# Early statistics beside two stages, layer 1 and rows of the first sample placed closer, and the values' row of layer 3 added in the context

## The chip, the core and the metric

The kernel runs on one core of a Trainium2 chip. The core has a matrix engine (TensorE, PE in the profile; its weight loads are shown apart as PEld), a vector engine (VectorE, DVE), an activation engine (ScalarE, ACT), a general engine (GpSimd, POOL) and a synchronization engine (SyncE, SP), which here only issues DMA transfers. Each engine works through its own list of instructions in order and waits on semaphores for the others. The metric is device time in microseconds of one execution.

## The reference, cut to what matters

The input x is 16 samples of 4096 tokens (64 x 64) with 256 channels, in float32. Four layers follow one another, each of the form x = x + layer(group norm of x), with 32 groups over channels and all tokens of a sample. So every layer needs a whole sample's statistics before it can begin.

```
layer 0: indices = argmin(|xf|^2 + |E|^2 - 2 xf E)        # 1024 codes; the code's vector is added
layer 1: f, g, h = x Wf, x Wg, x Wh (with biases); out = sigmoid(f g^T) h   # over the 64 positions of a row
layer 2: sim = x0[:, None] * x1[None, :]; sm = softmax(sim, axis=1)         # 4096 x 4096 a sample
         gate = sigmoid(x2 sm); out = gate * x
layer 3: q, k, v = split(x w_qkv); q = softmax over a head's 32; k = softmax over tokens
         context = k v^T; out = layernorm((context q) w_out + b_out) * gamma + beta
```

## The kernel before, in words

A sample goes through stages, each a Python generator that yields after a piece of work:

- stats0 (lines 313 to 324): loads the sample's transposed input in 8 chunks of 512 KB (line 319, pool xb, 4 buffers), BN_STATS on DVE (line 266, two a chunk), and at the end gn_finish (lines 276 to 299), a short chain over PE, ACT and POOL that gives scale and bias.
- stage1, "search" (lines 329 to 436): 32 tiles of 128 tokens. Its loads are lines 338 (pool xa) and 342. A tile is the code distances on PE (line 403), the row term on ACT (line 398), maximum and index on DVE (lines 409 and 414), and a gather-and-add DMA issued by POOL (line 415). Per chunk of four tiles the result is transposed on PE (line 378), copied by ACT (line 381), given to BN_STATS and stored (line 384).
- layer1 (lines 441 to 562): 8 chunks. Loads at line 453 (pool xm), PE lines 482, 493, 498, 513 and 533, the add on DVE (line 538), BN_STATS, store at line 545.
- rows2 (lines 567 to 608) and spread_rows (610 to 618): the three rows x0, x1, x2 of layer 2 (line 590 loads through pool xb, line 593 multiplies, line 599 stores the rows, line 615 spreads them to all partitions).
- stage2, "exps" (lines 620 to 676): 64 times an exponential of 128 x 2048 on ACT (line 645) and a multiply-and-sum on DVE (line 648). Then gate2 (lines 681 to 714, line 695 reads the gate back, line 703 applies it).
- stage3, "layer 3" (lines 717 to 926). Its first half computes keys (line 765), queries and values together (line 782, two tiles to a PSUM bank, 128 columns of queries and 128 of values each), adds the row qv_row (the group norm's mean carried through the weights, in three bfloat16 parts) with a matmul of ones (line 786), and accumulates the context ctxa = exp(k) v over the chunks (lines 807, 809, 813). After the last chunk come ksum (line 827, the sum of exp(k) per key channel) and the small chain from the transposed context (line 832) to the output weights (lines 834 to 852).

The order of the work has two layers. A table of tasks with a start, a length and a number of pieces (lines 932 to 958) is run through a heap (lines 961 to 968): each task's next piece is traced when its virtual time comes; one unit is one sample's search. FILL (line 39) says in which stretches the statistics of samples 1 to 7 are traced: two passes in 0.05 to 0.95, three in 1.0 to 1.27, two in 1.4 to 1.58. The constants LAG1, LEN1, LAGR, LAG2 place layer 1, rows and exps behind one another; for sample 0 layer 1 begins at 1.06 and has length 0.2, the rows have 0.1, the exps follow 0.17 later. The framework then schedules the traced instructions onto the engines' lists, with what stands under tc.high_priority (gn_finish and the small chains) drawn forward. What results is a fixed list for each engine, SP's list of DMA issues among them: a load that has to wait for its buffer holds up all loads behind it.

Of the kernel before, what the change touches and what calls it, by code (L numbers as in the profile page):

```python
# [2 lines left out]

# [32 lines left out]
LAG3, LENG = 0.06, 0.8  # L36
LAG4 = 0.04
LEN3 = {0: 0.4, 1: 0.33, 2: 0.37}
FILL = ((0.05, 0.95, 2), (1.0, 1.27, 3), (1.4, 1.58, 2))
EARLY = sum(n for _, _, n in FILL)  # L40


@with_exitstack
def kernel(
# [263 lines left out]
                engine.tensor_scalar(v, v, scale[:, k : k + 1], None, ALU.mult)  # L308


    norm0 = {}

    def stats0(b):
        tag = f"s0_{b}"
        st = stats_tile(0, f"st_{tag}")
        src = xT[b].rearrange("(k p) n -> p k n", p=P)
        for ch in range(NCHUNK):
            xt = xb.tile([P, NK, CW], F32, tag="xb", name=f"xs_{tag}_{ch}")
            nc.sync.dma_start(out=xt, in_=src[:, :, ch * CW : (ch + 1) * CW])
            chunk_stats(st, xt, ch)  # L320
            yield 1.5
        with tc.high_priority(offset=URGENT):
            norm0[b] = gn_finish(st, "n0", b)
        yield 2


    x1_d, norm1 = {}, {}

    def stage1(b):
# [5 lines left out]

        def load(ch):
            xt[ch] = xa.tile([P, NK, CW], F32, tag="xa", name=f"xt_{tag}_{ch}")
            nc.sync.dma_start(out=xt[ch], in_=src[:, :, ch * CW : (ch + 1) * CW])

        def tokens(ch):  # L340
            xc[ch] = s1p.tile([P, CH, C], F32, tag="xc", name=f"xc_{tag}_{ch}")
# [51 lines left out]
        for ch in range(NCHUNK):  # L393
            for t in range(CH):
                T = ch * CH + t

                nn = s1p.tile([P, CODES], F32, tag="t4", name=f"nn_{tag}_{T}", bufs=3)
                nc.scalar.activation(nn, ne2, AF.Identity, bias=nx2[ch][:, t : t + 1])  # L398
                pd = wide(f"pd_{tag}_{T}")
                for hf in range(2):  # L400
                    cols = slice(hf * 512, (hf + 1) * 512)
                    for k in range(NK):
                        nc.tensor.matmul(  # L403
                            pd[:, cols], lhsT=xn[ch][:, k, t * P : (t + 1) * P], rhs=e2[:, k, cols],
                            start=(k == 0), stop=(k == NK - 1),
                        )

                m8 = m8s[T % 4]
                nc.vector.tensor_tensor_reduce(  # L409
                    out=nn, in0=pd, in1=nn, scale=1.0, scalar=-3.0e38, op0=ALU.add, op1=ALU.max,  # L410
                    accum_out=m8[:, 0:1],
                )
                i8 = small.tile([P, 8], U32, tag="i8", name=f"i8_{tag}_{T}", bufs=4)
                nc.vector.max_index(i8, m8, nn)  # L414
                nc.gpsimd.indirect_dma_start(  # L415
                    out=xc[ch][:, t, :], out_offset=None,
                    in_=emb_rows, in_offset=bass.IndirectOffsetOnAxis(ap=i8[:, 0:1], axis=0),
                    compute_op=ALU.add,
                )
                yield 4  # L420
                if t == 1 and ch > 0:
                    back(ch - 1)
                    yield 2
                if t == 2 and ch + 1 < NCHUNK:
                    norm(ch + 1)
                    yield 2
                if t == 3:
                    if ch + 1 < NCHUNK:
                        norm_rows(ch + 1)
                        tokens(ch + 1)  # L430
                    if ch + 2 < NCHUNK:
                        load(ch + 2)
# [8 lines left out]
    def layer1(b):  # L441
# [8 lines left out]

        def load(ch):
            xt[ch] = xm.tile([P, NK, CW], F32, tag="xm", name=f"xt_{tag}_{ch}")
            nc.sync.dma_start(out=xt[ch], in_=x1[ch])

        load(0)
        load(1)
# [93 lines left out]
        for ch in range(NCHUNK):  # L550
            if ch > 0:
                store(ch - 1)
            if ch + 1 < NCHUNK:
                yield from attend(ch + 1)
                yield 2
            mix(ch)
            yield 3
        store(NCHUNK - 1)

# [157 lines left out]
    def stage3(b):  # L717
# [40 lines left out]
        for ch in range(NCHUNK):  # L758
# [18 lines left out]
            for pr in range(CH // 2):  # L777
                pqv = bank(f"pqv_{tag}_{ch}_{pr}").rearrange("p (j n) -> p j n", j=2)
                for j in range(2):
                    t = 2 * pr + j  # L780
                    for k in range(NK):
# [1 line left out]
                            pqv[:, j, :], lhsT=xt[:, k, t * P : (t + 1) * P], rhs=wqv_n[:, k, :],  # L783
                            start=(j == 0 and k == 0), stop=False, skip_group_check=True,
                        )
                nc.tensor.matmul(pqv, lhsT=ones3, rhs=twice(qv_row), start=False, stop=True, skip_group_check=True)
                nc.scalar.copy(qv[:, 2 * pr : 2 * pr + 2, :, :].rearrange("p j s n -> p j (s n)"), pqv)
            if ch == 0:
                put_row(x_row, xm_, by_identity, f"x_{tag}", idle=8)
# [39 lines left out]
        nc.vector.reciprocal(rk, ksum)  # L829
        with tc.high_priority(offset=URGENT):  # L830
            pt = bank(f"pct_{tag}")
            nc.tensor.transpose(pt[:, :P], ctxa, ident)
            ctx_bd = wts.tile([P, P], F32, tag="ctx_bd", name=f"ctxbd_{tag}")
            nc.vector.tensor_tensor(ctx_bd, pt[:, :P], hmask, ALU.mult)
# [95 lines left out]


    tasks, free = [], {}
    b = 0
    for begin, end, n in FILL:
        for k in range(n):
            b += 1
# [9 lines left out]
    for b in range(nb):  # L946
# [1 line left out]
        if b > EARLY:  # L948
            tasks.append((b - 0.7, 0.5, stats0(b), 14))
        task("search", b, 1.0, stage1(b), 160)  # L950
        end = task("layer1", b + 1 + LAG1, (LEN1 if b else 0.2) if left else 0.35, layer1(b), 88)
        task("rows", end + LAGR, 0.1, rows2(b), 8)
        if left:
            end = task("exps", end + LAG2, 1.0, stage2(b), 160)
            end = task("gate", end + LAG3, 0.15 if left == 1 else LENG, gate2(b), 36)
        else:
            end = task("exps", end + LAG2, 0.65, stage2(b, NCHUNK), 200)
# [47 lines left out]
```

## Time and profile before

| | |
|---|---|
| median of 3 runs | 5679.94 us (5666.18 to 5681.68) |
| profiled execution | 5674.06 us |
| its span, first to last instruction | 5672.1 us |
| mean granted TensorE clock | 0.962 |
| instructions | 76096 |
| DMA | 1059.26 MB, 187 GB/s over the span |

The page gives, for each engine, busy time, share of the span and number of instructions. Matmuls are pipelined, and their recorded ends are modelled, so a PE that is shown busy is not PE at its peak. Two more views are used. One cuts the span into stretches and gives each engine's busy time in them, with the granted clock, the mean busy share of the 16 DMA engines and what they moved. The other lists who waited for whom: engine, line, what released it, total us, times, longest us. An f32 matmul of the code stands in the trace as two records.

Where the stages of the first two samples stand in the profiled execution (first and last start of their main instructions, us):

| stage | sample 0 | sample 1 |
|---|---|---|
| search (DVE line 409) | 39 to 177 | 184 to 480 |
| layer 1 (DVE line 538) | 216 to 289 | 540 to 673 |
| rows (PE line 593) | 298 to 313 | 685 to 702 |
| exps (DVE line 648) | 333 to 590 | 718 to 1000 |
| layer 3, first half (PE line 765) | 831 to 987 | 1296 to 1436 |

### The profile page before, as it was taken

What the parts mean: (1) busy time and instruction counts of PE and PEld (TensorE: products, weight loads), DVE (VectorE), ACT (ScalarE), POOL (GpSimd) and SP (SyncE); (2) the same over time, 40 slices, a digit from 0 to 9 for tenths busy, and PEclk for the clock granted to TensorE, in tenths of its full rate; (3) what the DMA queues carried; (4) which work ended last, traced back from release to release, by engine and by line L of the source; (5) the groups of instructions that cost most, each with busy time, mean ns of one, the idle gap of its engine ahead of it and who ended that gap; (6) DMA issues with size and microseconds to landing.
All of it is one profiled execution on the core that took longest, in us unless ns stands there. A gap on an engine that the chain in (4) does not pass through costs nothing.

```text
span 5672.1 us, 76096 instructions
## 1 busy us (share of the span) xinstructions
PE 5162.0 (91%) x26927; PEld 3189.6 (56%) x26927; DVE 5049.3 (89%) x7186; ACT 4571.1 (81%) x6642; POOL 1801.5 (32%) x1076
## 2 busy tenths in 40 slices
PE   7977889989999999999999999999999999987788
PEld 3534446545656566565655656565565656564556
DVE  7589799899999999999999999999999999988882
ACT  4468589888989898888978888898888879887873
POOL 2223234323333333334333333333333333321221
PEclk9988999999999999999999999999999999998889
DMA  8553744655665757566575656657575675745543
GB/s 254 174 178 84 232 115 144 214 163 185 196 198 175 224 159 236 171 211 198 185 234 155 216 185 200 210 173 236 160 224 183 201 219 156 222 149 176 200 157 119
DMA packets 521365, 1059.26 MB, mean 187 GB/s; under 512 B 52504, under 2 KB 266392, under 8 KB 512792
## 3 DMA queue, kind: packets, MB, share of 16 engines
q1 hardware_dynamic: 406288, 885.11, 46.5%
q0 software_dynamic: 73728, 67.14, 8.3%
q10 hardware_dynamic: 40968, 102.13, 4.6%
q8 instruction: 214, 3.51, 0.3%
q14 instruction: 167, 1.37, 0.1%
HBM read 751.18 MB, written 303.04 MB: 186 GB/s over the span
## 4 chain that ended last, share of the span: by engine, by line
PE 46%; DVE 17%; ACT 16%; issue 6%; DMA 5%; POOL 4%; SPq 0%; ACTq 0%; DVEq 0%; POOLq 0%
PE pd_s L403 14%; ACT ex_s L645 7%; DVE ex_s L648 7%; PE ph_l L493 4%; PE pxo_s L908 3%; PE pqv_s L782 3%; PE po_l L533 2%; PE pk_s L765 2%; ACT nn_s L398 2%; POOL qv_s L802 2%; PE pz_s L857 2%; DVE i_s L414 2%; DVE nn_s L409 2%; PE pxo_s L902 2%; PE pvr_s L865 2%
## 5 line engine op out<-in xcount | busy, mean ns | idle before, releaser
L648 DVE CUSTOM_DVE_ANT_0 ex_s<-ex_s,x2b 128x2048 f32<-128x2048 f32 x1024 | 2360.4, 2312 | 77.6 <-ACT ex_s L645 74.6
L645 ACT ACTIVATE ex_s<-x0b,nmax_s,x_r 128x2048 f32<-128x2048 f32 x1024 | 2138.6, 2089 | 40.7 <-DVE num_s L648 30.5
L403 PE MATMUL pd_s<-e,xn_s 128*128 128x512 f32 x4096 | 1971.1, 614 | 43.9 <-DVE m L409 27.9
L415 POOL DMA_INDIRECT xc_s<-in_emb_rows,i_s x512 | 1113.7, 2175 | 1852.7 <-DVE i_s L414 1337.5
L403 PEld LDWEIGHTS pd_s<-e,xn_s 128*128 128x128 f32 x4096 | 745.8, 195 | 778.8 <-issue 669.1
L409 DVE CUSTOM_DVE_ANT_0 nn_s<-pd_s,nn_s 128x1024 f32<-128x1024 f32 x512 | 619.9, 1212 | 113.5 <-PE pd_s L403 63.0
L414 DVE FIND_INDEX8 i_s<-m,nn_s 128x8 uint32<-128x1024 f32 x512 | 622.9, 1217 | 0.0
L398 ACT ACTIVATE nn_s<-ne,nx_s 128x1024 f32<-128x1024 f32 x512 | 582.5, 1143 | 33.1 <-DVE nx_s L369 18.7
L493 PE MATMUL ph_l<-wh_l,xt_l 128*128 128x256 f32 x2048 | 519.6, 390 | 28.7 <-DVE m L409 16.9
L782 PE MATMUL pqv_s<-wqv_s,xk_s 128*128 128x256 f32 x2048 | 489.3, 381 | 0.0
L493 PEld LDWEIGHTS ph_l<-wh_l,xt_l 128*128 128x128 f32 x2048 | 379.7, 192 | 138.9 <-issue 69.0
L782 PEld LDWEIGHTS pqv_s<-wqv_s,xk_s 128*128 128x128 f32 x2048 | 389.1, 191 | 120.6 <-issue 59.7
L802 POOL TENSOR_TENSOR qv_s<-qv_s,qm_s 128x512 f32<-128x512 f32 x128 | 221.6, 1731 | 662.6 <-DVE qm_s L801 363.2
L868 POOL TENSOR_TENSOR lrs_s<-lrs_s,mhalf 128x4 f32<-128x4 f32 x128 | 178.0, 1391 | 677.2 <-ACT lrs_s L867 663.3
L756 POOL TENSOR_TENSOR qv_s<-qv_s,qd_s 128x512 f32<-128x512 f32 x128 | 214.4, 1675 | 249.0 <-DVE qd_s L755 132.0
L533 PE MATMUL po_l<-blk,h_l 128*128 128x128 f32 x2048 | 282.1, 288 | 3.0 <-DVE m L409 1.5
L533 PEld LDWEIGHTS po_l<-blk,h_l 128*128 128x128 f32 x2048 | 260.6, 200 | 41.1 <-issue 24.5
L908 PE MATMUL pxo_s<-wctx_s,qo_s 128*128 128x256 f32 x1024 | 269.2, 386 | 2.2 <-DVE qo_s L876 2.2
L765 PE MATMUL pk_s<-xk_s,wk_s 128*128 128x512 f32 x512 | 256.0, 620 | 1.0 <-DMA xk_s<-x_g 0.9
L913 ACT COPY y_s<-pxo_s 128x512 f32<-128x512 f32 x256 | 147.5, 580 | 132.4 <-PE pxo_s L912 116.0
L378 PE MATMUL pt_s<-ident,xc_s 128*128 128x128 f32 x1024 | 156.7, 282 | 105.2 <-DMA xc_s<-in_emb_rows,i_s 79.0
L351 ACT ACTIVATE sq_s<-xt_s,first 128x512 f32<-128x512 f32 x256 | 200.2, 806 | 37.2 <-DMA x0b<-rows_r 21.0
(206 smaller groups left out, 7322.0 us busy)
## 6 DMA issues: line engine op xcount, KB each, us to landing
xs_s<-in_xT SPq DMA_DIRECT2D x128, 512.0 KB
xt_s<-in_xT SPq DMA_DIRECT2D x128, 512.0 KB
xc_s<-in_x SPq DMA_DIRECT2D x128, 512.0 KB
x_s<-xt_s ACTq DMA_DIRECT2D x128, 512.0 KB
xt_l<-x_s SPq DMA_DIRECT2D x128, 512.0 KB
x_l<-xt_l SPq DMA_DIRECT2D x128, 512.0 KB
xr_r<-x_l SPq DMA_DIRECT2D x128, 512.0 KB
xg_g<-x_l SPq DMA_DIRECT2D x128, 512.0 KB
```

The source lines that it names most:

```text
L398: nc.scalar.activation(nn, ne2, AF.Identity, bias=nx2[ch][:, t : t + 1])
L403: nc.tensor.matmul(pd[:, cols], lhsT=xn[ch][:, k, t * P : (t + 1) * P], rhs=e2[:, k, cols], start=(k == 0), stop=(k == NK - 1),)
L409: nc.vector.tensor_tensor_reduce(out=nn, in0=pd, in1=nn, scale=1.0, scalar=-3.0e38, op0=ALU.add, op1=ALU.max, accum_out=m8[:, 0:1],)
L414: nc.vector.max_index(i8, m8, nn)
L415: nc.gpsimd.indirect_dma_start(out=xc[ch][:, t, :], out_offset=None, in_=emb_rows, in_offset=bass.IndirectOffsetOnAxis(ap=i8[:, 0:1], axis=0),
L493: nc.tensor.matmul(ph[:, t, :], lhsT=X[:, k, t * P : (t + 1) * P], rhs=wh_n[:, k, :], start=(t % 2 == 0 and k == 0), stop=False, skip_grou ...
L533: nc.tensor.matmul(po[:, m : m + P], lhsT=h[:, t, k * P : (k + 1) * P], rhs=at[:, t, :, :].rearrange("p r i -> p (r i)"), start=True, stop ...
L645: nc.scalar.activation(ex, x0b, AF.Exp, bias=nmax[:, T : T + 1], scale=x01[:, T, 1:2], accum_out=den[:, h, T : T + 1])
L648: nc.vector.tensor_tensor_reduce(out=ex, in0=ex, in1=x2b, scale=1.0, scalar=0.0, op0=ALU.mult, op1=ALU.add, accum_out=num[:, h, T : T + 1],)
L765: nc.tensor.matmul(pk, lhsT=wk_n[:, k, :], rhs=xt[:, k, :], start=(k == 0), stop=(k == NK - 1))
L782: nc.tensor.matmul(pqv[:, j, :], lhsT=xt[:, k, t * P : (t + 1) * P], rhs=wqv_n[:, k, :], start=(j == 0 and k == 0), stop=False, skip_group ...
L908: nc.tensor.matmul(px[:, j, :], lhsT=qT[:, t * P : (t + 1) * P], rhs=wctx[:, 1, :], start=False, stop=False, skip_group_check=True,)
```

## The change

It has three parts. First, the statistics of samples 1 and 2 are no longer traced by virtual time but piece by piece beside the search of sample 0, from within its loop over tiles, and those of samples 3, 4 and 5 beside layer 1 of sample 0, from within its loop over chunks. Their loads are traced under `issue_after(marks[...])`, where the mark is the last load that the search or layer 1 has issued: on SP they stand behind it. The statistics of samples 6 and 7 move from 1.4 to 1.58 to 2.62 to 3.04. Second, for sample 0 alone, layer 1 is placed at 1.02 with length 0.12, its rows get length 0.04, and the exps follow 0.08 behind them. Third, the matmul of ones that adds qv_row covers only the queries' 128 columns of each tile. The values' part of the row is added once, to the context: every value had the same row added, so the context gains ksum times that row. A matmul of ones spreads the row into the PSUM bank of the transposed context, and one DVE operation adds ksum times it to ctxa before the transposition.

```
-FILL = ((0.05, 0.95, 2), (1.0, 1.27, 3), (1.4, 1.58, 2))
-EARLY = sum(n for _, _, n in FILL)
+FILL = ((2.62, 3.04, 2),)
+BESIDE = (2, 3)
+EARLY = sum(BESIDE) + sum(n for _, _, n in FILL)
...
-    norm0 = {}
-
-    def stats0(b):
+    norm0, marks = {}, {}
+
+    def behind(name):
+
+        return tc.issue_after(marks[name]) if name in marks else nullcontext()
+
+    def stats0(b, after=None):
...
-            nc.sync.dma_start(out=xt, in_=src[:, :, ch * CW : (ch + 1) * CW])
+            with behind(after):
+                nc.sync.dma_start(out=xt, in_=src[:, :, ch * CW : (ch + 1) * CW])
...
+    beside = {
+        "search": chain.from_iterable(stats0(b, "search") for b in range(1, 1 + BESIDE[0]) if b < nb),
+        "layer1": chain.from_iterable(stats0(b, "layer1") for b in range(1 + BESIDE[0], 1 + sum(BESIDE)) if b < nb),
+    }
+
+    def advance(name, b, n):
+
+        for _ in range(n if b == 0 else 0):
+            next(beside[name], None)
...
-            nc.sync.dma_start(out=xt[ch], in_=src[:, :, ch * CW : (ch + 1) * CW])
+            marks["search"] = nc.sync.dma_start(out=xt[ch], in_=src[:, :, ch * CW : (ch + 1) * CW]).ins
...
                 yield 4
+                advance("search", b, ((T + 1) * 9 * BESIDE[0]) // NT - (T * 9 * BESIDE[0]) // NT)
...
-            nc.sync.dma_start(out=xt[ch], in_=x1[ch])
+            marks["layer1"] = nc.sync.dma_start(out=xt[ch], in_=x1[ch]).ins
...
             mix(ch)
+            advance("layer1", b, ((ch + 1) * 9 * BESIDE[1]) // NCHUNK - (ch * 9 * BESIDE[1]) // NCHUNK)
...
-                nc.tensor.matmul(pqv, lhsT=ones3, rhs=twice(qv_row), start=False, stop=True, skip_group_check=True)
+                nc.tensor.matmul(
+                    pqv[:, :, 0:P], lhsT=ones3, rhs=twice(qv_row)[:, :, 0:P], start=False, stop=True, skip_group_check=True
+                )
...
             pt = bank(f"pct_{tag}")
+            nc.tensor.matmul(pt[:, P : 2 * P], lhsT=ones3, rhs=qv_row[:, P:], start=True, stop=True)
+            nc.vector.scalar_tensor_tensor(ctxa, pt[:, P : 2 * P], ksum, ctxa, op0=ALU.mult, op1=ALU.add)
             nc.tensor.transpose(pt[:, :P], ctxa, ident)
...
-    b = 0
+    b = sum(BESIDE)
...
-        end = task("layer1", b + 1 + LAG1, (LEN1 if b else 0.2) if left else 0.35, layer1(b), 88)
-        task("rows", end + LAGR, 0.1, rows2(b), 8)
+        end = task("layer1", b + 1 + (LAG1 if b else 0.02), (LEN1 if b else 0.12) if left else 0.35, layer1(b), 88)
+        task("rows", end + LAGR, 0.1 if b else 0.04, rows2(b), 8)
...
-            end = task("exps", end + LAG2, 1.0, stage2(b), 160)
+            end = task("exps", end + (LAG2 if b else 0.08), 1.0, stage2(b), 160)
```

## The prediction

> **What bounds the kernel now.** I read the page's engine totals first, then the busy time by stretch, cut where a stage of an early sample begins or ends; the cuts are first and last starts of the stage's lines. Columns: stretch, its length, then busy us and (instructions) of PE, weight loads, DVE, ACT and POOL, then the granted clock, the DMA share and GB/s.
>
> ```profile
> PE 5162.0 (91%) x26927; PEld 3189.6 (56%) x26927; DVE 5049.3 (89%) x7186; ACT 4571.1 (81%) x6642; POOL 1801.5 (32%) x1076
> ```
>
> ```profile
> 39.00:177.00 138.00, 126.45 (x463) 58.89 (x462) 121.67 (x211) 67.24 (x89) 50.50 (x35) 0.99 0.84 243
> 177.00:290.00 113.00, 104.66 (x705) 68.19 (x704) 54.45 (x90) 51.27 (x99) 16.86 (x15) 0.95 0.49 153
> 290.00:333.00 43.00, 36.47 (x146) 16.15 (x145) 25.55 (x50) 15.59 (x28) 12.00 (x12) 0.93 0.84 290
> 333.00:590.00 257.00, 189.77 (x773) 95.91 (x772) 244.68 (x314) 210.98 (x254) 78.32 (x36) 0.87 0.37 105
> 590.00:718.00 128.00, 113.93 (x554) 59.09 (x553) 85.61 (x146) 67.64 (x104) 30.34 (x22) 0.97 0.80 253
> 718.00:1016.00 298.00, 278.16 (x1416) 162.97 (x1414) 272.30 (x378) 262.42 (x371) 103.63 (x55) 0.96 0.47 143
> ```
>
> The rows are: search of sample 0; its layer 1; its rows; its 64 exponentials; the gap to the second sample's exponentials; those. No one engine sets the pace. Search 0 is PE (92%) with DVE behind it (88%) and much DMA; layer 1 is PE (93%) while DVE is half idle; the exponentials of sample 0 are DVE (95%) while PE is starved; the gap is PE and DMA. From 718 on PE and DVE are both over 90% and a sample takes some 330 us. The start is where engines take turns in waiting; the steady part has little slack anywhere.
>
> How the order moves I read from the built programs' instruction orders. Tile (s,t) is the t-th of the 32 search tiles of sample s on DVE. Layer 1 of sample 0 (its eight chunk adds) stands behind tiles (1,2) to (1,7) before, behind (1,0) to (1,3) after. The first exponential product of sample 0 stands behind (1,13) before, behind (1,6) after; its last behind (2,11) before, (2,4) after. The first product of sample 1 stands behind (2,29) in both. From the second sample's layer 3 on both orders are the same but for part three. So the start is decided by when (2,29) is reached, 718 now.
>
> **Part 1, the early statistics.** Within search 0 DVE runs 60 of their BN_STATS before, 34 after (676 ns each by its rows): 26 x 0.68 = 17.6 us less of DVE's 121.7. This does not set the end there; PE does, and it can win only its idle 138 - 126.5 = 11.5 us. Two waits tell how much of that the statistics cause (window 40 to 177; who waited for what, total us, times, longest), and one of SP's own (0 to 700):
>
> ```profile
> ACT xn_s L348 <- DMA xt_s<-in_xT: 12.9, 5, 3.0
> PE pt_s L378 <- DMA xc_s<-in_emb_rows,i_s: 11.5, 7, 2.9
> ```
>
> ```profile
> SPq L319 <- DVE st_s L266: 97.7, 39, 7.6
> ```
>
> SP issues in order. A statistics load (L319) that waits for a buffer which DVE has to free holds up the search's own load (L338) behind it, and ACT then waits for that. After, each statistics load stands behind the search load just issued. The gathers (L415), for which PE waits, share the 84% DMA with 13 fewer statistics loads. I take half of the 11.5: **-6**; bounds 0 and -11.5.
>
> The passes of samples 3 to 5 move into layer 1: 42 BN_STATS there instead of 16, 26 x 0.68 = 17.6 us more, on a DVE busy 54 of 113 us, where PE hides them. Their loads are 13 x 0.52 MB = 6.8 MB more on 153 GB/s x 113 us = 17.3 MB. The passes of samples 6 and 7 leave the rows and exponentials of sample 0 (8 in front of the first product, 24 behind it, 32 x 0.68 = 21.7 us of a saturated DVE) and go to tiles (2,4) to (2,31), where DVE is busy 86 of 128 us.
>
> **Part 2, layer 1 and rows closer.** Layer 1 loses four tiles of filler. A tile costs PE 8 records 0.43 us apart and some 0.4 us of transposes and row sums (L378: 156.7 us for 512 tiles), 3.8 us: 113 - 15 = 98. Its 24.1 MB less 2 MB of tiles in 98 us are 225 GB/s; the highest of the rows above is 290, so it fits, but SP's loads and stores of a chunk (L453, L545) now have statistics loads ahead of them that wait for buffers. I put 6 us on that (bounds 0 and 24, a 3 us landing wait per chunk as the longest 3.0 above): 104, **-9**. The rows' stretch is a chain of round trips: last BN_STATS 288.7, row matmuls 298 to 313, spread rows, first exponential on ACT at 322.3. Fewer search tiles inside it do not shorten it. Only the 10 us between 322.3 and DVE's first product at 332.7, spent on BN_STATS of sample 6 and search tiles, goes: **-10**. Exponentials begin at 333 - 6 - 9 - 10 = 308.
>
> The exponentials' stretch holds 30 tiles in both orders. DVE's 244.7 loses 24 BN_STATS (16.2) and three chunk adds of sample 1's layer 1 with their statistics (1.21 + 2 x 0.68 each, 7.7): 221, at 95% 232 us. End at 540, where it was 590.
>
> What is late next is PE. The gap to (2,29) now holds 25 tiles where it had 18, and eight chunks of layer 1 where it had five. A chunk costs PE 16 x 0.216 + 2 x 0.216 + 16 x 0.112 and about 1.7 for the small matmuls, 7.3 us. That is 7 x 3.8 + 3 x 7.3 = 48 us more: 176 us at the old 89% busy, and the 50 us are given back (540 + 176 = 716). With no exponentials beside layer 1, the nearest row is 177 to 290, PE 93% busy: 169 us, second exponentials at 709, **-9** on 718. Bounds: 716, and 690 if PE also loses the gate's round trip that the chain of waits shows at 598 to 618. DMA leaves little more: 253 x 128 us = 32.4 MB, plus 3.7 for tiles, 3.1 for chunks, 6.8 for 13 statistics loads is 46 MB, 159 us at the 290 GB/s of the row above.
>
> The Trainium skill, "DMA: Bandwidth & Descriptors", section Bandwidth, measures 425 GB/s for a core alone with large transfers; by that estimate the 46 MB take 108 us, DMA bounds nothing there, and the sum would be up to 19 us lower. No stretch of this trace reaches that rate.
>
> Behind 718, layer 3 of sample 0 starts eight tiles or so earlier; the work moves from a stretch where DVE bounds (1016 to 1312: DVE 281, PE 266 of 296) into one where PE is 93% busy. I cost it at 0, bounds +10 and -8.
>
> **Part 3, the values' row.** 256 matmuls of 512 columns become 256 columns. In the order of time (start, us, engine, line) the next matmul starts 0.21 us behind one:
>
> ```profile
> 836.89 0.38 PE L786 MATMUL pqv_s<-qv_row,ones 128*128 128x512 bf16 x1
> 837.10 0.81 PE L782 MATMUL pqv_s<-wqv_s,xk_s 128*128 128x256 f32 x3
> ```
>
> The 0.38 is its latency, the 0.21 what it costs in a stream; half of 0.215 (the other rows' spacing) is 0.108 saved, 27.5 us in all. How much of that shows depends on what else is full. Busy time in the nine stretches from the first to the last start of L765, layer 3's first half, samples 0 to 8:
>
> ```profile
> sum 1300.00, PE 1237.77 PEld 762.88 DVE 1193.06 ACT 1143.03 POOL 474.54; mean PE 137.53 PEld 84.76 DVE 132.56 ACT 127.00 POOL 52.73
> ```
>
> PE 95%, DVE 92%, ACT 88%: PE is the fullest, not the only one. I count three quarters: -21. Added per sample: a 128-column matmul (0.05 us, a quarter of 0.215, to 0.33, the latency of L832) and one DVE operation:
>
> ```profile
> L809 DVE SCALAR_TENSOR_TENSOR ctx_s<-ctx_s,al_s,pc_s x112: 325/342/350, 871.4 to 5614.9; 128x128 f32<-128x128 f32 x112
> ```
>
> It has the same form as the new one: 16 x 0.34 = 5.5 us of DVE, and the transposition of the context (L832) now waits for it with search matmuls queued behind it on PE, and DVE's L409 behind those. It waits for ksum, which is ready. I put +3 on it, bounds 0 and +12 (16 x (0.34 + 0.38)). **Sum -18**, bounds -27 and +12 if PE's saving is hidden.
>
> The Trainium skill ("Trainium Kernel Development and Optimization", Best Practices) judges PE by the share of weight loads, not of matmuls; in those nine stretches that is 762.9 of 1300, 59%. By that rule PE has room, the saving is hidden, and the part is worth about +3.
>
> **Sum.** -9 - 18 = -27 on the profiled execution's 5674.1 (span 5672.1 and 2 around it): 5647. The median of the three runs shown, 5679.9, lies 6 above it; I set the forecast midway between the two footings, **5650**.
>
> **Rivals.** (a) The gap keeps PE's waiting down: second exponentials at 690, -28, and part three whole, -27 + 3: 5674 - 52, about 5622. For: DVE is freed of 24 us in its saturated stretch. Against: DMA at 80% already. (b) The start gives all back (716 or later) and part three is half hidden or wholly: 5663 to 5680. For: PE's work to (2,29) is the same in both orders, only idle time can be won. (c) Slower: layer 1 of sample 0 is set by its transfers. If its 22.1 MB run at 175 GB/s it takes 126 us; the exponentials begin at 333 - 6 + 13 - 10 = 330, the gap ends at 330 + 232 + 176 = 738, +20, the earlier layer 3 adds its +10 and part three is hidden, +3: about 5707. It decides from 196 GB/s downward (22.1 MB in more than 113 us). For: the stage runs at 153 now, and SP waits for buffers. Against: 243 GB/s in search 0. That the change does not do what it says is excluded: the built order shows every statistics load behind its search load.
>
> **Numbers.** Forecast case 0.48, (a) 0.14, (b) 0.23, (c) 0.15. The 8-in-10 range is 5615 to 5690. What a measurement tells from no change here is 0.3%, 17 us: faster means under 5663. The forecast case lies under it mostly (0.44 of 0.48), (a) wholly, (b) hardly (0.01): faster 0.59. Slower, over 5697, is most of (c): 0.13. The rest is 0.28.
>
> **What would show it.** Search 0 ends near 171 and ACT's waits for L338's loads shrink; the first exponential product at about 308, the last at 540, DVE 95% between; sample 1's first product at 709 (690: rival a; 716 or more: b or c); DMA in the gap at 250 to 290 GB/s; the values' row 0.108 us apart and PE's busy share in layer 3's first half one point lower with the stretch 1 to 2 us shorter. Wrong if layer 1 of sample 0 takes over 113 us, or if steady samples keep their present distance.

## The result, and the profile after

The changed kernel is slower. Its median is 5719.6 us (six runs, 5713.4 to 5733.4) beside 5681.1 us for the kernel before (six runs); the ratio is 1.0071, 95% interval 1.0057 to 1.0085. The forecast was 5650 us with a range of 5615 to 5690: the change went the other way, and the time lies above the range. The profiled execution of the changed kernel has a span of 5715.3 us, 43 more than before.

The engine totals of the changed kernel, in the same form as before:

```profile
PE 5160.3 (90%) x26943; PEld 3178.4 (56%) x26943; DVE 5065.6 (89%) x7202; ACT 4560.5 (80%) x6642; POOL 1822.4 (32%) x1076
```

PE, DVE and ACT are the old ones within 0.4%, POOL has 1.2% more. The 27.5 us that the halved matmul of ones was to save do not show in PE's total. PE stands idle 555 us where it was 510: the 43 us are waiting. Where it sits is told by the busy time by stretch, cut at the same events as before: search, layer 1, rows and exponentials of sample 0, the gap, and then from the first exponential product of sample 1 to that of sample 2, and on to that of sample 3. Columns: stretch, length, PE, weight loads, DVE, ACT, POOL with instructions, granted clock, DMA share, GB/s.

```profile
41.00:175.00 134.00, 124.44 (x452) 58.06 (x451) 107.65 (x187) 66.63 (x87) 49.29 (x33) 0.99 0.67 185
175.00:279.00 104.00, 94.01 (x660) 63.34 (x659) 55.83 (x91) 43.10 (x90) 11.63 (x14) 0.93 0.62 207
279.00:316.00 37.00, 34.62 (x118) 12.98 (x119) 13.52 (x30) 8.85 (x18) 7.27 (x9) 0.91 0.66 216
316.00:540.00 224.00, 158.88 (x538) 73.16 (x530) 221.76 (x273) 201.81 (x230) 80.43 (x32) 0.87 0.35 95
540.00:720.00 180.00, 170.05 (x882) 92.37 (x880) 128.48 (x222) 94.23 (x151) 42.95 (x34) 0.98 0.80 254
720.00:1035.00 315.00, 289.79 (x1535) 177.34 (x1536) 283.99 (x389) 261.68 (x376) 113.86 (x59) 0.96 0.49 151
1035.00:1338.00 303.00, 257.75 (x1265) 145.58 (x1263) 277.86 (x371) 256.46 (x343) 80.42 (x44) 0.91 0.55 173
```

The first five rows add up to what they were (720 against 718): the exponentials of sample 0 end 50 us earlier, and the gap takes the 50 us back, with PE busy 94% of it. The last two rows are new losses, 315 where it was 298 and 303 where it was 296. The row before that answers to the last one is

```profile
1016.00:1312.00 296.00, 266.43 (x1388) 156.76 (x1388) 280.69 (x376) 257.94 (x350) 88.01 (x47) 0.95 0.60 189
```

Some 120 PE records (a part of layer 3 of sample 0) have gone from this stretch into the one ahead of it. The one ahead grew by 17 us, and this one, relieved, did not shrink.

First exponential product of a sample, from the profiled executions (us; search 0 and the exponentials of sample 0 by their first start and last end, here and in the table of before, where the last start lies 1 to 2 us earlier; the second row is the kernel before profiled once more, run e12, to show how far two executions differ):

| kernel | search 0 | sample 0 | sample 1 | 2 | 3 | 5 | 7 | 13 |
|---|---|---|---|---|---|---|---|---|
| before | 39 to 177 | 333 to 590 | 718 | 1016 | 1312 | 1955 | 2623 | 4633 |
| before again | 42 to 181 | 338 to 597 | 726 | 1028 | 1324 | 1971 | 2642 | 4655 |
| after | 41 to 175 | 316 to 540 | 720 | 1035 | 1338 | 2007 | 2685 | 4685 |
| part one alone (e3) | 39 to 171 | 335 to 572 | 706 | 1012 | 1307 | 1958 | 2632 | 4640 |
| part two alone (e4) | 39 to 177 | 316 to 558 | 732 | 1045 | 1345 | 1992 | 2660 | 4672 |
| e7 | 38 to 174 | 321 to 563 | 736 | 1039 | 1337 | 1985 | 2654 | 4661 |
| e8 | 41 to 179 | 357 to 600 | 713 | 1010 | 1311 | 1958 | 2630 | 4643 |

Two executions of one kernel differ by up to 22 us at a late stage, so single stage times are read only where they differ by more, or agree over several kernels.

### The profile page after: what moved, and what is told of

It reads as the page before. It is cut to its first block, busy times and chain, and to the rows that moved or that the text cites. A ratio compares the mean times of both kernels' runs of the same rounds, so it can differ in the third digit from the quotient of the medians.

```text
span 5715.3 us, 76199 instructions
## 1 busy us (share of the span) xinstructions
PE 5160.3 (90%) x26943; PEld 3178.4 (56%) x26943; DVE 5065.6 (89%) x7202; ACT 4560.5 (80%) x6642; POOL 1822.4 (32%) x1076
## 4 chain that ended last, share of the span: by engine, by line
PE 49%; DVE 18%; ACT 14%; DMA 7%; issue 6%; POOL 5%; ACTq 0%; SPq 0%; DVEq 0%; POOLq 0%
PE pd_s L420 16%; DVE ex_s L667 7%; ACT ex_s L664 6%; PE ph_l L511 5%; PE pxo_s L931 3%; PE pqv_s L801 3%; DVE i_s L431 3%; PE po_l L551 2%; PE pk_s L784 2%; POOL qv_s L823 2%; DVE nn_s L426 2%; PE pxo_s L925 2%; PE pz_s L880 2%; ACT nn_s L415 2%; DMA qo_s<-qd_s 2%
## 5 line engine op out<-in xcount | busy, mean ns | idle before, releaser
L432 POOL DMA_INDIRECT xc_s<-in_emb_rows,i_s x512 | 1158.3, 2262 | 1886.8 <-DVE i_s L431 1288.1
L823 POOL TENSOR_TENSOR qv_s<-qv_s,qm_s 128x512 f32<-128x512 f32 x128 | 208.5, 1629 | 655.1 <-DVE qm_s L822 465.1
L395 PEld LDWEIGHTS pt_s<-ident,xc_s 128*128 128x128 f32 x1024 | 120.8, 145 | 193.6 <-DMA xc_s<-in_emb_rows,i_s 115.5
```

Source lines behind the costliest of these rows:

```text
L432: nc.gpsimd.indirect_dma_start(out=xc[ch][:, t, :], out_offset=None, in_=emb_rows, in_offset=bass.IndirectOffsetOnAxis(ap=i8[:, 0:1], axis=0),
```

## The experiments

Each ratio is to the kernel before, run beside it on the same chip, with its 95% interval.

### The parts alone

**e1, part three alone:** the kernel before with the two edits of layer 3.

```
-                nc.tensor.matmul(pqv, lhsT=ones3, rhs=twice(qv_row), ...)
+                nc.tensor.matmul(pqv[:, :, 0:P], lhsT=ones3, rhs=twice(qv_row)[:, :, 0:P], ...)
...
+            nc.tensor.matmul(pt[:, P : 2 * P], lhsT=ones3, rhs=qv_row[:, P:], start=True, stop=True)
+            nc.vector.scalar_tensor_tensor(ctxa, pt[:, P : 2 * P], ksum, ctxa, op0=ALU.mult, op1=ALU.add)
             nc.tensor.transpose(pt[:, :P], ctxa, ident)
```

> The kernel before with the third part alone (the values' row added in the context). Theory A (the loss of 39 us is the start's order, above all that sample 0's layer 3 and exponentials stand earlier): the third part is worth what the steady samples of the changed kernel show, 0 to -18 us on 5681, so 5663 to 5681. Theory B (the third part itself costs, by the wait of the context's transposition and of the row chains behind it): 5695 or more, with the distance from the exponentials of sample 3 to those of sample 5 grown from 643 us to over 660.

Measured: 5695.5, 1.0040 (1.0024 to 1.0057); from sample 3's exponentials to sample 5's 671 us. This is what theory B said.

**e2, the changed kernel without part three** (the same edit undone).

> The changed kernel without the third part: the statistics and the sample 0 placement stay. Theory A: as slow as the changed kernel or slower, 5715 to 5740; the exponentials of sample 2 start near 1035, those of sample 5 near 2005. Theory B: 5680 to 5700.

Measured: 5709.9, 1.0067 (1.0045 to 1.0089), between the two theories. Sample 2 begins at 1037 as theory A had it, sample 5 at 1991 and not near 2005.

**e3, part one alone:** the statistics beside search 0 and layer 1, the lags as before. **e4, part two alone:** the lags.

```
-        end = task("layer1", b + 1 + LAG1, (LEN1 if b else 0.2) if left else 0.35, layer1(b), 88)
-        task("rows", end + LAGR, 0.1, rows2(b), 8)
+        end = task("layer1", b + 1 + (LAG1 if b else 0.02), (LEN1 if b else 0.12) if left else 0.35, layer1(b), 88)
+        task("rows", end + LAGR, 0.1 if b else 0.04, rows2(b), 8)
...
-            end = task("exps", end + LAG2, 1.0, stage2(b), 160)
+            end = task("exps", end + (LAG2 if b else 0.08), 1.0, stage2(b), 160)
```

> The kernel before with the first part alone (statistics of samples 1 to 5 beside search and layer 1, 6 and 7 at 2.62). Theory A, if the exponentials' earlier place is the cause: 5670 to 5685, since the order of exponentials, gate and layer 3 of sample 0 is the old one. A rival within A, that the passes of samples 6 and 7, now in the gap before the exponentials of sample 1, cost: 5695 or more.

> The kernel before with the second part alone (layer 1, rows, exponentials of sample 0 placed closer; statistics as before). Theory A: slow by itself, 5700 to 5725, with the exponentials of sample 1 at about 718 to 725 and the loss between there and sample 5. Rival (statistics are the cause): 5675 to 5690.

Measured: e3 5668.0, 0.9978 (0.9960 to 0.9995); e4 5704.2, 1.0073 (1.0045 to 1.0101). e3 is 2 us faster than theory A had it. e4's time is in theory A's range, but sample 1 begins at 732, later than expected, and between samples 3 and 5 nothing is lost (647 us, where the two executions of before have 644 and 647). So the statistics gain a little, and parts two and three each lose when they stand alone. The three alone add up to +0.91%, the whole is +0.71%. They are not additive: the changed kernel is only 0.04% above e2, with intervals of 0.14% and 0.22% to either side. So part three, which costs 0.40% alone, is not seen on top of the other two, and most of the change's loss is there without it.

### Part two taken apart

**e7:** part two, with the gate of sample 0, and layer 3 behind it, at its old virtual time. **e8:** part two, with the exponentials and all behind them at their old virtual time; only layer 1 and rows are closer.

```
e7  +            end = task("gate", end + (LAG3 if b else 0.33), ...)
e8  +            end = task("exps", end + (LAG2 if b else 0.35), 1.0, stage2(b), 160)
```

> The second part alone, but gate and layer 3 of sample 0 at their old virtual time; layer 1, rows and exponentials are closer. If the earlier layer 3 is what costs between the exponentials of samples 1 and 3: the +20 us that the second part alone loses there go, 5685 to 5695. If the early exponentials cost: 5700 or more, as the second part alone.

> The second part alone, but the exponentials of sample 0, and all behind them, at their old virtual time: only layer 1 and rows are closer. If early exponentials or layer 3 cost: 5672 to 5685, as before. If the closer layer 1 itself costs: 5695 or more.

Measured: e7 5690.2, 1.0025 (1.0007 to 1.0043); e8 5678.0, 0.9997 (0.9978 to 1.0015). Both times are where the first theory had them. The closer layer 1 costs nothing and gains nothing that these intervals show; the early exponentials cost some 0.25%; the early gate and layer 3 the rest, about 0.5%.

Why early exponentials bring nothing is in the stretches. First the exponentials of sample 0 and the gap in e4, then in e8:

```profile
317.00:558.00 241.00, 159.59 (x531) 75.40 (x532) 236.21 (x304) 199.13 (x233) 74.12 (x37) 0.80 0.37 101
558.00:732.00 174.00, 163.91 (x865) 89.62 (x864) 113.54 (x190) 91.82 (x146) 38.52 (x28) 0.98 0.75 233
```

```profile
357.00:601.00 244.00, 185.29 (x772) 94.82 (x770) 237.97 (x298) 214.58 (x260) 76.56 (x35) 0.89 0.36 101
601.00:713.00 112.00, 102.06 (x493) 52.27 (x494) 77.64 (x137) 59.58 (x92) 26.28 (x20) 0.98 0.84 263
```

The exponentials last as long in both, since DVE sets them (236 of 241, 238 of 244). What differs is what lies under them on PE: 772 records in e8, 531 in e4. In e4 PE stands idle 81 us there, in e8 59, and the records that are missing turn up in the gap, where PE is 94% busy and each one costs time. From the start of search 0 to sample 1's exponentials PE's busy time is the same in both (578 and 576 us); only its idle time differs.

### Part three taken apart

**e5, the half width alone:** the matmul of ones covers the queries only, nothing is added to the context (the values lack their row, a part of the computation left out). **e6, the chain alone:** full width, and the two new instructions with a row of zeros, so that they change no value.

> The kernel before with the matmul of ones cut to the queries' half and nothing in its place: the values lack their row, which leaves that part of the computation out. Theory A (the added chain behind the context costs): the 0.108 us a matmul come back, 5655 to 5670. Theory B (the shorter matmul moves the built order of the other instructions, and that order costs between samples 3 and 5): 5690 to 5700, with the distance between the exponentials of samples 3 and 5 at about 670 us where it was 643.

> The kernel before with full-width matmuls, and the new matmul and DVE operation on a row of zeros in the chain. Theory A (the chain costs): 5690 to 5705. Theory B (the order): nothing of the chain's 0.4 us a sample is seen beyond 7 us, 5678 to 5690, unless its own order differs.

Measured: e5 5661.8, 0.9970 (0.9953 to 0.9988); e6 5731.4, 1.0103 (1.0069 to 1.0138). The saving on PE is there, 17 us by the ratio, near what I had counted (21); the next matmul follows at 0.109 us where it was 0.216 (median of 256). e5's time is theory A's, but from sample 3 to sample 5 it takes 661 us where the kernel before has 644 and 647, so a part of what theory B said is in it too. The chain costs 58 us by the ratio (51 between the medians), 26 us above theory A's range, where I had 3 and at most 12 in the prediction.

**e9:** the chain's two instructions behind the transposition, into a tile that nobody reads: the work without the wait.

```
             nc.tensor.transpose(pt[:, :P], ctxa, ident)
+            nc.tensor.matmul(pt[:, P : 2 * P], lhsT=ones3, rhs=zero_row[:, P:], start=True, stop=True)
...
             nc.vector.tensor_tensor(ctx_bd, pt[:, :P], hmask, ALU.mult)
+            nc.vector.scalar_tensor_tensor(beside_, pt[:, P : 2 * P], ksum, ctxa, op0=ALU.mult, op1=ALU.add)
```

> The kernel before with the chain kernel's matmul of ones on a row of zeros and its DVE operation, once a sample, but behind the transposition of the context and into a tile that nobody reads: the same work for PE and DVE, and no wait for it on the way to the output weights. Theory A, the added wait costs (the transposition, and everything queued behind it on PE, waits for a matmul and a DVE operation): the loss of 1.0% goes, ratio 0.998 to 1.003. Theory B, the wait costs little, and what costs is that two more instructions under high priority shift the planner's order of the work behind them: ratio 1.006 to 1.012.

Measured: 5695.5, 1.0021 (1.0008 to 1.0035). That is in theory A's range: the two instructions cost 0.7% and more only where the transposition stands behind them. It does not yet show that the waiting is the cost, since e9 and e6 differ in the order of other instructions too (below).

**e17:** the chain of e6 with a constant column (eps3) in place of ksum. **e18:** e1 with the four operations that make ksum and its reciprocal under the chain's high priority.

> The chain kernel (matmul of ones on a row of zeros and DVE operation in front of the context's transposition), with the DVE operation's factor taken from a constant column instead of ksum: the two operations stay in the chain, the wait for ksum goes. Theory A, the wait for ksum is the cost (the transposition starts 1.5 us ahead of the reciprocal of ksum in the kernel before, 2.0 us behind it with the chain): ratio to the kernel before 1.000 to 1.004, transposition ahead of the reciprocal again. Theory B, two more links in the chain cost whatever they wait for: 1.007 to 1.013.

> The kernel before with part three as in the changed kernel, and the four operations that make ksum and its reciprocal under the same high priority as the chain, so that ksum is there earlier. Theory A, the wait for ksum is part three's loss (1.004 without this): ratio 0.996 to 1.000. Theory B: 1.003 to 1.007.

Measured: e17 5718.7, 1.0074 (1.0055 to 1.0093); e18 5700.1, 1.0034 (1.0019 to 1.0049), where e1 had 1.0040. In e17 the transposition runs ahead of ksum's reciprocal in 10 of 16 samples, as in 12 before, and in e18 ksum is ready 9 us and more ahead of its use in the first 13 samples. So the wait for ksum is not the cause; theory A falls. The two instructions cost with or without it.

What a link is, the order of time around the context of one sample shows, first before, then e6 (start, us, engine, line, operation):

```profile
3109.83 0.33 PE L832 MATMUL pct_s<-ident,ctx_s 128*128 128x128 f32 x1
3110.20 0.29 DVE L834 TENSOR_TENSOR ctxbd_s<-pct_s,hmask 128x128 f32<-128x128 f32 x1 [1.25 <-PE pct_s L832]
3110.57 0.10 DVE L827 TENSOR_REDUCE ksum_s<-fac_s 128x1 f32<-128x8 f32 x1
```

```profile
3145.75 0.10 DVE L828 TENSOR_REDUCE ksum_s<-fac_s 128x1 f32<-128x8 f32 x1
...
3146.43 0.23 PE L833 MATMUL pct_s<-zero_row,ones 128*128 128x128 bf16 x1
...
3146.96 0.34 DVE L834 SCALAR_TENSOR_TENSOR ctx_s<-pct_s,ksum_s,ctx_s 128x128 f32<-128x128 f32 x1
3146.97 1.98 PE L404 MATMUL pd_s<-e,xn_s 128*128 128x512 f32 x4
...
3148.79 0.27 PE L835 MATMUL pct_s<-ident,ctx_s 128*128 128x128 f32 x1
```

The reader is to see two things. In this sample ksum was not ready before: the transposition ran ahead of it, as in 10 of the 16 samples (it is behind it in the first three and the last three). And the instructions of 0.23 and 0.34 us take 3.0 us from ksum to the transposition, the largest piece being the 1.5 us from the end of the DVE operation to the start of the transposition on PE. PE is not idle in these 1.5 us: it runs the search's matmuls (L404), which the order has put ahead. Where it has none, in the last four samples, the transposition starts 0.06 us after the DVE operation. Ahead of the transposition PE idles 3.0 us before, 8.4 in e6 and 4.5 in e17, summed over 16 samples; ahead of all PE instructions from there to the gram matrix (L850 of the kernel before) 21.6 us before, 26.6 in e6, 21.9 in e17.

The whole path from the last addition to the context to the gram matrix in SBUF (L852) is, on the mean of 16 samples:

| before | again | e9 | e6 | e17 | e18 | after |
|---|---|---|---|---|---|---|
| 17.4 | 17.6 | 17.4 | 18.4 | 17.6 | 16.4 | 17.4 |

16 samples times 1.0 us, 16 of the 58, would be the most that it explains in e6, and in e17, e18 and the changed kernel it is no longer than before. So the time is not lost on this path itself. What else differs is the order in which the engines run. In the two executions of the kernel before, DVE and ACT run their instructions in the same order. Of their 7186 and 6642, some 60 and 120 stand elsewhere in e9, 110 and 170 in e6, 90 and 140 in e17, and 490 and 460 in e5, which gains: it is not the number of moved instructions that costs.

**Where the rest sits.** The two stretches from the exponentials of sample 3 to those of sample 5, in four kernels: before again, e9, e6, and the changed kernel.

```profile
1324.00:1651.00 327.00, 314.25 (x1672) 195.79 (x1671) 304.26 (x428) 283.80 (x412) 112.25 (x64) 0.98 0.61 189
1651.00:1971.00 320.00, 308.61 (x1672) 192.44 (x1671) 304.02 (x428) 283.62 (x412) 113.66 (x64) 1.00 0.63 194
```

```profile
1317.00:1644.00 327.00, 313.26 (x1673) 194.76 (x1672) 304.27 (x427) 283.79 (x412) 113.71 (x64) 0.98 0.61 189
1644.00:1969.00 325.00, 311.10 (x1675) 193.33 (x1674) 304.60 (x431) 284.14 (x412) 113.55 (x64) 0.99 0.61 191
```

```profile
1318.00:1651.00 333.00, 314.54 (x1675) 194.94 (x1674) 305.49 (x429) 283.84 (x412) 111.70 (x64) 0.98 0.59 186
1651.00:1986.00 335.00, 315.20 (x1675) 195.77 (x1674) 305.18 (x431) 283.93 (x412) 112.52 (x64) 0.97 0.59 185
```

```profile
1338.00:1673.00 335.00, 314.67 (x1675) 194.23 (x1674) 307.31 (x431) 283.82 (x412) 111.77 (x64) 0.98 0.59 185
1673.00:2007.00 334.00, 313.45 (x1672) 193.88 (x1671) 306.12 (x429) 282.91 (x411) 114.76 (x64) 0.98 0.59 185
```

And e5, which has the half width and no chain:

```profile
1325.00:1654.00 329.00, 312.19 (x1672) 193.26 (x1671) 305.70 (x426) 283.00 (x412) 115.58 (x64) 0.98 0.61 188
1654.00:1986.00 332.00, 314.29 (x1673) 194.44 (x1673) 306.67 (x430) 283.41 (x412) 112.87 (x64) 0.98 0.60 187
```

The kernels with the chain take 668 and 669 us, before again and e9 647 and 652, the first profile of before 643. The other chain kernels show it too (e1 671, e13 668, e17 666, e18 668, e15 671). But e5 takes 661, and e10, e11 and e16 below, with the half width and nothing in the chain, 659 to 662. So the longer stretch is no mark of the chain: the half width alone has over half of it, and is as fast as before or faster on the whole. Waits of these stretches (who waited for what, total us, times, longest), before again, then e6:

```profile
DVE nn_s L409 <- PE pd_s L403: 4.1, 6, 1.1
...
ACT lrs_s L867 <- PE pvr_s L865: 1.9, 8, 0.3
...
ACT top_qv_s L156 <- PE prow_qv_s L163: 0.4, 2, 0.2
```

```profile
DVE nn_s L410 <- PE pd_s L404: 11.6, 7, 2.6
ACT top_qv_s L157 <- PE prow_qv_s L164: 11.1, 2, 5.6
ACT lrs_s L870 <- PE pvr_s L868: 9.7, 8, 4.2
...
PE pt_s L379 <- DMA xc_s<-in_emb_rows,i_s: 7.0, 2, 3.5
...
PE pz_s L860 <- DMA qo_s<-qd_s: 5.7, 2, 3.0
```

In e6 PE waits for a gather (7.0) and for the queries read back (5.7), neither of which before again has in these stretches, and others wait for PE. In e9 the waits of nn and lrs are as large as in e6 (12.3 and 10.2), though it loses little; but those for the gather and the queries are 0.6 and 3.0, and that of top_qv is 0.3. e5 has neither the chain nor its loss, and these two lines:

```profile
ACT top_qv_s L156 <- PE prow_qv_s L163: 9.5, 2, 5.0
PE pt_s L378 <- DMA xc_s<-in_emb_rows,i_s: 7.4, 2, 3.9
```

So the gather and top_qv go with the longer stretch, and not with the loss of the whole kernel. Only PE's wait for the queries read back is left as a mark of the chain (none in e5, 4.0 to 5.7 in the chain kernels), and it is small. That is a reading of single executions, not a proof.

### A theory that fell: SP's queue

In e1, e6 and the changed kernel SP's load of the search's tokens (L342) waits up to 18.6 us for PE's transpositions to free its buffer, with the queries' reads behind it; from 1312 to 2623 us these waits make 66 to 68 us, in the kernels without the chain 27 to 48. A third buffer for that tile takes the reason away and leaves the compute engines' orders almost as they are.

```
-            xc[ch] = s1p.tile([P, CH, C], F32, tag="xc", name=f"xc_{tag}_{ch}")
+            xc[ch] = s1p.tile([P, CH, C], F32, tag="xc", name=f"xc_{tag}_{ch}", bufs=3)
```

e13 is e6 with it, e14 the kernel before with it, e15 the changed kernel with it.

> The chain kernel (matmul of ones on a row of zeros and DVE operation in front of the context's transposition) with three buffers in place of two for the search's token tile xc; the orders of PE, DVE, ACT and POOL stay, SP's loads of xc come free earlier. Theory A, the loss of 1.0% comes from SP, whose load of xc waits up to 17.5 us for PE and holds up the reads of layer 3's queries behind it: ratio to the kernel before 0.998 to 1.004, the wait of that load in samples 3 to 7 under 30 us. Theory B, the loss is in the compute engines' order or in the chain's wait itself: ratio 1.007 to 1.013.

> The control: the kernel before with three buffers for xc. Theory A: little of SP's waiting for xc holds up anything here, ratio 0.996 to 1.001. Theory B, the buffer helps any kernel by as much: ratio 0.988 to 0.994, and e13 then stays 1% above it.

> The changed kernel with three buffers for xc. Theory A: part three's loss of about 0.4% goes, and the early exponentials and layer 3 of the first sample keep theirs (0.7%) against the statistics' gain (0.2%): ratio 1.001 to 1.005. Theory B: 1.006 to 1.009 as without.

Measured: e13 5727.6, 1.0077 (1.0058 to 1.0096); e14 5687.6, 1.0009 (0.9997 to 1.0022); e15 5712.4, 1.0057 (1.0040 to 1.0074). With the buffer on both sides the chain still costs 0.7%, as theory B had it; e15 lies between the two. In e13 the load still waits 61.5 us in that window: the planner issues it earlier, and it waits as before. So the lack of a buffer is not the main cause. Since the wait itself stayed, it is not excluded as a link, but nothing shows it to be one.

### The values' row without a chain, and better versions

**e10:** half width, with the row put into the bias of the output weights. Divided by ksum, the row's share of the context no longer depends on the keys: it is a matmul of (hmask times the row) with wo, added to bo four chunks and more ahead of its use. **e11:** e3 with e10. **e16:** e11 with three buffers for xc. **e12:** the kernel before, once more.

```
+            if ch == 2:
+                nc.tensor.matmul(pvb[:, 0:1], lhsT=qv_row[:, P:], rhs=ones3[:, 0:1], start=True, stop=True)
+                nc.scalar.copy(vcol, pvb[:, 0:1])
+                nc.gpsimd.tensor_scalar(hrow, hmask, vcol, None, ALU.mult)
+            if ch == 3:
+                nc.tensor.matmul(pvb[:, :C], lhsT=hrow, rhs=wo, start=True, stop=True)
+                nc.vector.tensor_tensor(bo_b, pvb[:, :C], bo, ALU.add)
```

> The kernel before with part three in another form: the matmul of ones covers the queries' half only, and the values' row goes into the bias of the output weights (the row as a column, hmask times it, a matmul with wo, an addition to bo), done during chunks 2 and 3, five chunks ahead of its use, so that nothing stands in the chain between the last chunk and the output weights. If the chain was part three's loser, this keeps the half width's gain of 0.3% less some 5 us for four operations a sample: 5655 to 5672, ratio 0.996 to 0.999. Rival: any added instruction in layer 3 costs by the shift of the order: ratio 1.002 to 1.006.

> Part one (early statistics beside search 0 and layer 1 of sample 0) with the values' row in the bias, no other change to the kernel before. If the two gains are separate: 0.9978 and 0.996 to 0.999 together, 5645 to 5668, ratio 0.994 to 0.998. Rival: the parts are not additive since each changes the order of the steady samples: ratio 1.000 to 1.006.

> Early statistics, the values' row in the bias and three buffers for xc, nothing of part two. Theory A: the half width's gain, which its own disturbance of SP's queue took back (43 to 48 us of waits for xc in samples 3 to 7 against 27 to 34), shows: ratio 0.992 to 0.996. Theory B: as without the buffer, 0.9975.

> The kernel before once more, unchanged, for a second profile of it: how far two executions differ by stage. In the first, the exponentials of samples 1, 2, 3 and 7 begin at 718, 1016, 1312 and 2623 us. Theory: differences of 10 us between two kernels' stages mean nothing, those of 30 us do: sample 7 begins at 2610 to 2640. Rival: the loss of 30 us that the changed kernels show between samples 3 and 7 lies within what the kernel before shows by itself: sample 7 at 2640 or later.

Measured: e10 5681.3, 0.9998 (0.9988 to 1.0008); e11 5667.8, 0.9975 (0.9965 to 0.9985); e16 5667.8, 0.9976 (0.9963 to 0.9988); e12 one time, 5687.0, sample 7 at 2642. In e10 nothing is in the chain, and the half width's gain is given back all the same: its time lies between what theory and rival had. e11 is where I had expected it, but e11, e16 and e3 cannot be told apart, so what gains there is part one, and the third buffer shows nothing. These three are the fastest complete kernels of the study. Why e10 gives the gain back is not shown. e12 at 2642 is on the rival's side by 2 us: differences of up to 22 us between two kernels' late stages mean nothing.

## Why the prediction was wrong

**Bounds of the stages: right.** The stages alternate between PE and DVE as read, and the first four stretches came out near their numbers: search 0 lost 4 us (I had 6), layer 1 of sample 0 takes 104 us (104), the exponentials begin at 316 (308) and end at 540 (540). The last is in part luck: they begin 8 us late and last 8 us less than I had, with DVE 99% busy and not 95%. The two waits that the 6 us of search 0 were read from hardly shrank (ACT's for the search's load from 12.9 to 11.3 us, PE's for the gathers from 11.5 to 9.6), so how its 4 us came is not shown. "From 718 on PE and DVE are both over 90%" holds up to 4960 us only; nothing in the sum rests on it. The transfers kept up: layer 1 ran at 207 GB/s and the gap at 254, so rival (c), whose time of 5707 lies nearest, did not happen by its mechanism.

**The gap: the term was mis-sized.** I had 169 us at PE 93% busy and sample 1 at 709. It is 180 us at 94%, sample 1 at 720. PE's busy time there is 170.05 us, 56 more than before, where I had counted 48 and then added busy time to length: 114 + 48 us of PE at 93% are 174 us, not 169. So 11 us, and the gain of 9 became a loss of 2 us: rival (b) for this part. The reason is the one that e4 and e8 show: sample 1 starts when PE's work is done, and early exponentials only take away the work under which PE was idle.

**"Layer 3 of sample 0 starts eight tiles or so earlier ... I cost it at 0, bounds +10 and -8": this step failed.** From sample 1's first product to sample 3's the changed kernel takes 618 us, e2 621 (722 to 1343) and e4 613, before 594, before again 598: +15 to +27, above the upper bound. The runs that keep layer 3 of sample 0 at its place take 592 to 609. I had named the right move, from a stretch bound by DVE into one full on PE, and not drawn the sum: in the full one PE has 12 us more to do and the stretch is 17 us longer, and in the other DVE's 278 us stay, so nothing comes back. e7, which has the early exponentials but not the early layer 3, loses 0.25% where e4 loses 0.73%. With the two steps together parts one and two lose 0.67% (e2), 38 us, where I had a gain of 9.

**Part three: the saving was right, the chain was not.** The half width gives 17 us of the 21 counted. The Trainium skill ("Trainium Kernel Development and Optimization", Best Practices) judges how far PE is from its roofline by its use of peak FLOP/s (MFU) and its share of weight loads, and not by matmul busy time. I had read the share, 59% here, as room that hides the saving; e5 shows 0.30% (0.12 to 0.47), so here it was not hidden, though in e10 it is gone again. "I put +3 on it, bounds 0 and +12 (16 x (0.34 + 0.38))" failed twice. "It waits for ksum, which is ready" is false in the trace of before for 10 of 16 samples, and I could have seen it there: the transposition starts ahead of L827. But e17 and e18 show that this is not what costs. And the bound was made of the durations of the two instructions: by the ratios the chain costs 58 us in e6 and 42 in e17, 2.6 to 3.6 us a sample, and 12 us (e9) where the transposition does not stand behind them. Longer waits on the path do not make up the difference either, since in e17 the path is as long as before.

**"From the second sample's layer 3 on both orders are the same but for part three": true, and I drew nothing from it.** From sample 3's first product on DVE and ACT run in the order of before in e2, e3 and e4; in e1 and the changed kernel over 300 instructions of each stand elsewhere. I counted part three as work and not as a change of the order. That its loss comes from the order is not shown.

**What stays open.** That the two instructions cost 0.5 to 0.8% more ahead of the transposition than behind it is shown by e6, e17 and e9, and that early exponentials and an early layer 3 of sample 0 make up part two's loss by e4, e7 and e8. By what way the chain costs is not settled: the lack of a buffer and ksum are excluded as its main cause, and the path to the gram matrix is not longer in e17, e18 and the changed kernel. What is left is the shifted order of the other instructions and the transfers that PE then meets too early; the half width shifts the order more and gains. A run with the old order forced on the chain kernel was not made. Why part three adds 0.40% to the kernel before and only 0.04% to e2 is open too.

## What to carry to other kernels

When work is moved, ask first what it was lying under. Here PE's work under the exponentials, where PE idled, cost little; in a stretch where PE was full it cost its busy time and more, while the stretch it left got no shorter, since another engine set it. Do not price a new link in a planned order by the duration of its instructions: here the durations make 9 us (16 x (0.23 + 0.34)), the loss was 42 to 58, and it did not lie on the link's own path. Move such an addition, and then measure: small edits of layer 3 were worth from -0.3% to +1.0% here. With differences under 1%, profile the unchanged kernel twice before reading stages, and look for the sign of a loss in a kernel that does not lose, as e5 here.

## What was not expected of the hardware

The granted TensorE clock goes with PE's small waits even where PE is over 90% busy: in the pair of stretches above before again has 0.98 and 1.00, the first profile of before 1.00 and 0.99, e6 0.98 and 0.97, and PE's busy time for nearly the same records (1672 and 1675) is 308.6 us at a clock of 1.00 and 315.2 at 0.97. Under the exponentials of sample 0 it is 0.87 before with PE 74% busy, 0.80 in e4 with 66%, and 0.87 in the changed kernel with 71%. If it is the waits that lower the clock, which no run here separates, a wait costs twice, once as idle time and once in the matmuls around it. The page "TensorE: Matmul & The Clock Gate" of the Trainium skill (Part 1) has the gate at half or full only; the rows here are means over 300 us and cannot tell a mixture from a value between.

The highest rate of a stretch was 290 GB/s before and 287 in e3's gap; no stretch that was cut here came near the 425 GB/s that the prediction set against it, and none was shown to be bound by its transfers.
